# Turning tiles one step ahead, reordering a weight's first sums, and seven block products per expert

## The chip, the cores and the metric

The kernel runs on one core of one Trainium2 chip. The metric is the device time of one launch in microseconds (us). A core has five engines that run side by side, each with its own instruction queue: TensorE (PE) does matrix products and transpositions into PSUM, VectorE (DVE) does elementwise work, ScalarE (ACT) does activations, copies and scalings, GpSimd (POOL) issues the indirect DMAs, and SyncE (SP) issues most of the other DMAs. An engine works through its queue in order; a wait for another engine or a DMA holds everything behind it in that queue.

## What is computed

A state x of 625 tokens by 1024 goes through four layers, each added to x behind a layer norm: a graph layer with eight relations and a gate, a quantized linear layer, a graph convolution, and a mixture of eight experts (top 2) with a shared expert. Cut to what the change touches:

```python
# layer 1: x @ root is the first matrix product of the kernel
out = x @ root + bias
for r in range(8):
    out = out + mean[r] @ weight[r]
...
# layers 2 and 3
acc = x_int8 @ weight_int8.T
h = einsum('nd,od->no', x, W) + b
...
# layer 4
logits = x @ router_w
expert_in = einsum('nec,nh->ech', dispatch, x)
hmid = silu(einsum('ech,ehf->ecf', expert_in, w1) + b1[:, None, :])
expert_out = einsum('ecf,efh->ech', hmid, w2) + b2[:, None, :]
y = einsum('nec,ech->nh', combine, expert_out)
shared = silu(x @ sw1 + sb1) @ sw2 + sb2
out = y + 0.1 * shared
```

An expert has 196 slots, 1024 inputs, 256 hidden values and 1024 outputs; all of this is float32.

## The kernel before

The 625 tokens are five tiles of 125 rows. PE contracts over partitions, so each tile is first turned (`transposed`: eight 128-column blocks in two groups of four; each group goes to a PSUM tile of a ring of two, and ACT copies it to SBUF). Products go to a ring of four PSUM tiles (`mm_tile`), each of which is free again when its reader, on DVE or ACT, is done.

The program is written with a scheduler behind it. It keeps PE's steps in the written order (`issue_after`, `in_steps`), but on the other engines it takes, at each moment of its own planned time, the earliest written instruction that is ready; so a later one can fill a gap. `behind(d, e)` puts d after e on an engine without a wait.

The matrix products of layer 1 use seven block products in place of eight (Winograd's form of Strassen's scheme). A weight is four blocks of 512 by 512, two tiles are a pair, and for a pair `combine_rows` makes the row sums s1, s2, s4 (and puts one difference in place), `combine_weights` makes t1 = b12 - b11, t2 = b22 - t1, t4 = b21 - t2, and `last_weight` puts b22 - b12 in place of b12. The seven products and the sums out of PSUM are in `tile_pair`; the odd fifth tile goes through plain products in `tile_alone`. `posted` lists the DVE operations that must not be overtaken: the weight sums stand behind the last of them. For the root weight, the first one, `combine_rows(0)` stands ahead of `combine_weights` and fills `posted` first. All later units (seven relations, the gate, the last relation) call `combine_weights` and `last_weight` in `unit`. While they run, DVE counts edges and POOL adds the counts to a table in HBM; SP zeroes that table (three transfers of 3 MB at 31.5 us) and loads the weights in a fixed order.

Layers 2 and 3 are steps on PE: `quantized(t)` is the product of layer 2 for tile t with its layer norm on DVE, `columns(t)` turns tile t and multiplies it by W. `neighbours(t)` is the sum over edges with the next norm on DVE, `router(t)` turns tile t and forms its logits. A step that turns a tile and multiplies it at once has PE waiting for the copy on ACT. Then come the slots (which token goes where), the shared expert's output (`shared_out`, five tiles, whose sums go to X and on to `out` through SP), and the experts.

For each expert e: POOL gathers the tokens of its slots (`gather`, two indirect DMAs of 98 rows); PE turns them (`turn`), both halves one after the other; `expert_hidden` is two groups of eight products of 196 columns with an activation on ACT; `expert_out` is 2 by 2 blocks (98 slots by 512 columns) of two accumulated products, one DVE operation each with the gate and the bias that ACT has scaled by the gate (`b2g`), and a store for each 98 slots, an indirect DMA on POOL that adds to `out`. A store waits for those of the previous expert, since it may add to the same rows. Before the change turn(e+1) follows the hidden layer of e and precedes its output. Weights of expert e+3 are loaded when their slot comes free, and `ye`, which the stores read, has two buffers.

Of the kernel before, what the change touches and what calls it, by code (L numbers as in the profile page):

```python
# [8 lines left out]
F32 = mybir.dt.float32  # L9
# [4 lines left out]
AF = mybir.ActivationFunctionType  # L14
# [32 lines left out]
def layers(  # L47
# [383 lines left out]
    def combine_weights(b):  # L431

        t1, t2, t4 = (tp.tile([128, 4, HC], F32, tag=f"t{i}", name=f"t{i}") for i in (1, 2, 4))
        for o, v, w in ((t1, b[0][1], b[0][0]), (t2, b[1][1], t1), (t4, b[1][0], t2)):
            d = nc.vector.tensor_sub(o, v, w)  # L435
            if posted:
                behind(d, posted[-1])
        return t1, t2, t4
# [54 lines left out]
    def last_weight(b):  # L493

        nc.vector.tensor_sub(b[0][1], b[1][1], b[0][1])
# [31 lines left out]
    combine_rows(0)  # L527
    root_t = combine_weights(root_w)
# [432 lines left out]

    def columns(t):
        transposed(xT, t * P, th[t], P)
        for h in range(2):
            hs = slice(h * HC, (h + 1) * HC)
            ps = mm_tile()
            for k in range(KD):
                last = nc.tensor.matmul(  # L968
                    ps[:P, :],
                    xT[:, k, t * P : (t + 1) * P],  # L970
                    gcn_w[h][k // 4][:, k % 4, :],
                    start=(k == 0),
                    stop=(k == KD - 1),
                )
            z = work.tile([P, HC], F32, tag="z", name="z")
            nc.vector.tensor_add(z, ps[:P, :], gcn_b_row[:, hs])
            nc.scalar.mul(parts[t][0][:, hs], z, dis[:, t : t + 1])
            if not exact:
                hi, lo = (v[:, hs] for v in parts[t])
                nc.vector.scalar_tensor_tensor(  # L980
                    lo, z, dis[:, t : t + 1], hi.bitcast(F32), op0=ALU.mult, op1=ALU.subtract
                )
        return last

    for step, t in ((quantized, 0), (quantized, 1), (quantized, 2), (columns, 0), (quantized, 3),
                    (columns, 1), (quantized, 4), (columns, 2), (columns, 3), (columns, 4)):
# [74 lines left out]
    def router(t):  # L1061
        transposed(xT, t * P, th[t], P)
# [37 lines left out]
    def in_steps(steps):  # L1100
        nonlocal pe_last
        for step, arg in steps:
# [5 lines left out]
            (neighbours, 0), (neighbours, 1), (neighbours, 2), (router, 0), (neighbours, 3),  # L1108
            (router, 1), (neighbours, 4), (router, 2), (shared_hidden, (0, 0, 3 * P)),
            (router, 3), (router, 4), (logits, None), (shared_hidden, (1, 0, 3 * P)),  # L1110
# [124 lines left out]
    done, base = sent, []  # L1235

    def shared_out(t):
        for h in range(2):
            hs = slice(h * HC, (h + 1) * HC)
            ps = mm_tile()  # L1240
            for f in range(2):
# [9 lines left out]
            nc.vector.scalar_tensor_tensor(  # L1251
                X[t][:, hs], z, 0.1, X[t][:, hs], op0=ALU.mult, op1=ALU.add
# [11 lines left out]
    in_steps([(shared_out, t) for t in range(NT)])  # L1264
# [36 lines left out]
    def turn(e):  # L1301
        for j in range(2):
            last = transposed(tiles["xeT"][e % 2], j * CP, rows_of_slots(e, j), CP)
        return last

    def expert_hidden(e):
        for f in range(2):
            ps = mm_tile()
            for k in range(KD):
                last = nc.tensor.matmul(  # L1310
                    ps[:, :CAP],
                    weights[e][0][:, k, f * 128 : (f + 1) * 128],
                    tiles["xeT"][e % 2][:, k, :],
                    start=(k == 0),
                    stop=(k == KD - 1),
                )
            nc.scalar.activation(
                tiles["he"][e % 2][:, f, :], ps[:, :CAP], AF.Silu, bias=b1_sb[:, e, f : f + 1]
            )
        return last  # L1320

    sent = base

    def expert_out(e):
        nonlocal sent
# [3 lines left out]
        for j in range(2):  # L1329
# [3 lines left out]
            for h in range(2):  # L1333
# [13 lines left out]
                in_halves = e == NE - 1 and j == 1  # L1347
                if h == 0 and not in_halves:
                    continue

                if in_halves:
                    to, v, rows = out.rearrange("n (h c) -> (n h) c", h=2), ye[:, j, hs], 2 * N
                    at = bass.IndirectOffsetOnAxis(ap=half_i[:, h : h + 1], axis=0)
                else:
                    to, v, rows, at = out, ye[:, j, :], N, rows_at(j, e, token_i)
                d = nc.gpsimd.indirect_dma_start(  # L1356
                    out=to,
                    out_offset=at,
                    in_=v,
                    in_offset=None,  # L1360
                    bounds_check=rows - 1,
                    oob_is_err=False,
                    compute_op=ALU.add,
                )
                for o in sent:
                    tc.declare_no_dep(d.ins, o.ins, reason="a token has one slot of an expert")
                after(d, earlier)
                sent.append(d)
        return last

    gather(0)
    for e in range(4):
        load_weights(e)
        load_bias(e)
    gather(1)
    in_steps(((turn, 0),))
    for e in range(NE):
# [5 lines left out]
        in_steps(((expert_hidden, e),))  # L1383
        if e + 2 < NE:
            gather(e + 2)
        in_steps((*(((turn, e + 1),) if e + 1 < NE else ()), (expert_out, e)))
# [58 lines left out]
```

## Time and profile before

| | us |
|---|---|
| median of three runs (1214.35 to 1215.61) | 1215.44 |
| the profiled execution | 1218.88 |
| its span on the core | 1217.1 |

| stage (us from the span's start) | what runs |
|---|---|
| 0 to 84 | tile norms and the root weight |
| 84 to 641 | eight relations and the gate |
| 641 to 835 | sums over edges |
| 835 to 1010 | gate, layers 2 and 3 |
| 1010 to 1068 | sums over edges, router |
| 1068 to 1094 | slots, shared expert's output |
| 1094 to 1217 | eight experts |

How to read the profile: a line in order of time has its start, its duration, the engine, the line of the kernel, the operation, what it writes and reads by name, the shapes and a count of merged instructions; in brackets stands the idle time before it and what ended it. A product in float32 appears as two records. PEld is the loading of PE's stationary operand. A line of waits has the total, the number and the longest. A line of a stretch has its length, the busy time and count of PE, PEld, DVE, ACT and POOL, the clock that TensorE was granted (1.00 is full speed), and the DMA's busy share and GB/s.

### The profile page before, as it was taken

What the parts mean: (1) busy time and instruction counts of PE and PEld (TensorE: products, weight loads), DVE (VectorE), ACT (ScalarE), POOL (GpSimd) and SP (SyncE); (2) the same over time, 40 slices, a digit from 0 to 9 for tenths busy, and PEclk for the clock granted to TensorE, in tenths of its full rate; (3) what the DMA queues carried; (4) which work ended last, traced back from release to release, by engine and by line L of the source; (5) the groups of instructions that cost most, each with busy time, mean ns of one, the idle gap of its engine ahead of it and who ended that gap; (6) DMA issues with size and microseconds to landing.
All of it is one profiled execution on the core that took longest, in us unless ns stands there. A gap on an engine that the chain in (4) does not pass through costs nothing.

```text
span 1217.1 us, 10940 instructions
## 1 busy us (share of the span) xinstructions
PE 1183.8 (97%) x3770; PEld 647.6 (53%) x3770; DVE 836.4 (69%) x1292; ACT 172.8 (14%) x308; POOL 485.5 (40%) x224
## 2 busy tenths in 40 slices
PE   6899999999999999999999999999999999999996
PEld 3344444444444444444447888786445447756663
DVE  5789797888897979793427888874998516451111
ACT  2000000000000000000013122213321111213331
POOL 1003888888787889888700000002420000013322
PEclk9999999999999999999999999999999999989998
DMA  8986737373646364636347779804540006269962
GB/s 274 268 232 153 204 60 202 65 196 74 183 85 174 88 178 92 155 70 149 50 106 197 172 192 257 218 1 115 147 142 17 18 26 212 82 213 267 284 156 43
DMA packets 156009, 177.05 MB, mean 145 GB/s; under 512 B 78831, under 2 KB 95590, under 8 KB 155946
## 3 DMA queue, kind: packets, MB, share of 16 engines
q1 hardware_dynamic: 66082, 132.03, 37.5%
q0 software_dynamic: 72864, 12.01, 10.3%
q10 hardware_dynamic: 17000, 32.24, 8.5%
q8 instruction: 32, 0.52, 0.2%
q14 instruction: 31, 0.25, 0.1%
HBM read 131.66 MB, written 45.50 MB: 146 GB/s over the span
## 4 chain that ended last, share of the span: by engine, by line
PE 92%; DMA 2%; ACT 2%; DVE 1%; issue 1%; POOL 1%; POOLq 0%; ACTq 0%; DVEq 0%
PE mm L442 51%; PE mm L684 15%; PE mm L968 6%; PE mm L812 6%; PE mm L1337 3%; PE mm L1310 2%; PE mm L996 2%; PE mm L1242 2%; PE mm L945 1%; PE mm L1079 1%; PE tr L186 1%; DMA out_dram<-aT,token_i 1%; ACT xT L189 1%; PE lgT L1066 1%; POOL out_dram L1356 1%
## 5 line engine op out<-in xcount | busy, mean ns | idle before, releaser
L400 POOL DMA_INDIRECT table<-hits,idx x165 | 409.6, 2483 | 195.7 <-DMA table<-zero 103.4
L442 PE MATMUL mm<-w,xT 128*125 128x512 f32 x800 | 351.1, 593 | 0.0
L376 DVE SCALAR_TENSOR_TENSOR junk<-kr,key,wm 125x1375 f32<-125x1375 f32 x165 | 271.5, 1646 | 1.1
L442 PEld LDWEIGHTS mm<-w,xT 128*125 128x125 f32 x800 | 150.3, 188 | 192.4 <-issue 190.0
L684 PE MATMUL mm<-hi,b 125*125 125x512 f32 x400 | 157.8, 394 | 0.0
L442 PE MATMUL mm<-t,btot 128*125 128x512 f32 x320 | 145.6, 598 | 4.5 <-DVE t L435 4.5
L684 PE MATMUL mm<-y,b 125*125 125x512 f32 x350 | 138.7, 396 | 0.0
L442 PEld LDWEIGHTS mm<-t,btot 128*125 128x125 f32 x320 | 60.6, 189 | 83.2 <-issue 77.7
L1294 POOL DMA_INDIRECT th<-tokens,token_i x16 | 16.2, 1010 | 208.7 <-DMA w<-in_L_ffn_w_dram 171.2
L1018 POOL IOTA io<- 125x40 f32 x1 | 0.2, 198 | 225.2 <-ACT th L794 225.2
L745 DVE SCALAR_TENSOR_TENSOR X<-mm,rc,X 125x512 f32<-125x512 f32 x80 | 60.0, 751 | 38.7 <-PE mm L684 37.9
L684 PEld LDWEIGHTS mm<-hi,b 125*125 125x125 f32 x400 | 74.2, 186 | 18.4 <-issue 0.2
L684 PEld LDWEIGHTS mm<-y,b 125*125 125x125 f32 x350 | 64.9, 185 | 15.8
L442 PE MATMUL mm<-w,btot 128*125 128x512 f32 x160 | 71.9, 592 | 0.0
L442 PE MATMUL mm<-t,xT 128*125 128x512 f32 x160 | 71.9, 592 | 0.0
L968 PE MATMUL mm<-w,xT 128*125 128x512 f32 x160 | 70.0, 595 | 1.4 <-ACT xT L189 1.4
L812 PE MATMUL mm<-w,xT 128*125 128x512 f32 x160 | 69.1, 592 | 0.0
L560 ACT CAST hi<-y 125x512 fp32r<-125x512 f32 x80 | 44.1, 617 | 159.8 <-PE mm L684 113.3
L1337 PE MATMUL mm<-w,th 128*98 128x512 f32 x128 | 56.3, 592 | 0.0
L461 ACT COPY y<-mm 125x512 f32<-125x512 f32 x18 | 10.6, 586 | 299.9 <-PE mm L442 292.1
L435 DVE TENSOR_TENSOR t<-w,t 128x2048 f32<-128x2048 f32 x20 | 45.8, 2290 | 6.9 <-DMA w<-in_L_gnn_weight_dram 6.5
L442 PEld LDWEIGHTS mm<-t,xT 128*125 128x125 f32 x160 | 29.9, 188 | 38.2 <-issue 37.7
(207 smaller groups left out, 1197.0 us busy)
## 6 DMA issues: line engine op xcount, KB each, us to landing
w<-in_L_gnn_weight_dram SPq DMA_DIRECT2D x32, 1024.0 KB
w<-in_L_ffn_w_dram SPq DMA_DIRECT2D x16, 1024.0 KB
yd<-y ACTq DMA_DIRECT2D x70, 224.0 KB
y<-yd SPq DMA_DIRECT2D x70, 224.0 KB
table<-zero SPq DMA_DIRECT2D x4, 3054.0 KB
b<-table SPq DMA_DIRECT2D x8, 1367.2 KB
kr<-key_rows ACTq DMA_DIRECT2D x15, 601.6 KB
w<-in_L_gnn_w_gate_dram SPq DMA_DIRECT2D x8, 1024.0 KB
```

The lines of the kernel that those rows point to most:

```text
L376: d = nc.vector.scalar_tensor_tensor(junk, kr, key[:, c : c + 1], wm[:, (EG - 1 - j) * P : (2 * EG - 1 - j) * P], op0=ALU.is_equal, op1=AL ...
L400: d = nc.gpsimd.indirect_dma_start(out=table, out_offset=bass.IndirectOffsetOnAxis(ap=idx[:, c : c + 1], axis=0), in_=hits[:, c : c + 1], ...
L435: d = nc.vector.tensor_sub(o, v, w)
L442: last = nc.tensor.matmul(ps[:P, :], lhs[:, k], rhs[:, k], start=(start and k == 0), stop=(stop and k == 3))
L560: upper.append(nc.scalar.copy(hi, y))
L684: last = nc.tensor.matmul(ps[:P, :], counted[r][:, k, t * P : (t + 1) * P], part, start=(k == ks[0] and part is parts[r, h, k][0]), stop=( ...
L745: nc.vector.scalar_tensor_tensor(X[at][:, hs], v[:P, :], rc[:, r, at : at + 1], X[at][:, hs], op0=ALU.mult, op1=ALU.add,)
L812: last = nc.tensor.matmul(ps[:P, :], xT[:, 4 * i + k, t * P : (t + 1) * P], gate_w[h][i][:, k, :], start=(i == 0 and k == 0), stop=(i == 1 ...
L968: last = nc.tensor.matmul(ps[:P, :], xT[:, k, t * P : (t + 1) * P], gcn_w[h][k // 4][:, k % 4, :], start=(k == 0), stop=(k == KD - 1),)
L996: last = nc.tensor.matmul(ps[:P, :], aT[:, k, t * P : (t + 1) * P], part[:, h * HC : (h + 1) * HC], start=(k == 0 and part is parts[k][0]) ...
L1242: last = nc.tensor.matmul(ps[:P, :], hT[:, f, t * P : (t + 1) * P], sw2_w[:, f, hs], start=(f == 0), stop=(f == 1),)
L1337: last = nc.tensor.matmul(ps[:CP, :], he[:, f, j * CP : (j + 1) * CP], weights[e][1][:, f, hs], start=(f == 0), stop=(f == 1),)
```

## The change

At the root weight, t1 and t2 are written ahead of the row sums of the first pair, so that they stand behind nothing posted; t4 and the last weight sum stay behind the row sums. In every unit, the last weight sum is now also written behind the last posted operation.

In layers 3 and 4, turning a tile becomes a step of its own, and is written one step ahead of the product that reads it, except for the first. Tiles 2 and 3 of the router are turned one after the other.

Expert 0's gather is written ahead of the shared output, and its two turns among the tiles of that output. Each later expert's turn is split: one half behind each half of the hidden layer before it.

The output of experts 0 to 6 uses seven block products: four blocks of the hidden values (two halves of the slots by two halves of the 256) and four of w2 (two halves of 256 by two of 1024). The weight sums (`expert_sums`) are made once an expert is done for the next, behind the last DVE operation of the shared output, in two sets of buffers in xT, which is free by then. ACT copies the first product out of PSUM, DVE makes three sums, and each of the four output blocks takes two DVE operations (`gated`), one of which reads PSUM. Both scaled biases are made first. The second half of the slots is stored first. Expert 7 keeps the old form, its second half stored in two parts as before.

```diff
-    def combine_weights(b):
+    def combine_weights(b, beside=None):
         t1, t2, t4 = (tp.tile([128, 4, HC], F32, tag=f"t{i}", name=f"t{i}") for i in (1, 2, 4))
         for o, v, w in ((t1, b[0][1], b[0][0]), (t2, b[1][1], t1), (t4, b[1][0], t2)):
+            if o is t4 and beside is not None:
+                combine_rows(beside)
             d = nc.vector.tensor_sub(o, v, w)
...
-        nc.vector.tensor_sub(b[0][1], b[1][1], b[0][1])
+        behind(nc.vector.tensor_sub(b[0][1], b[1][1], b[0][1]), posted[-1])
...
-    combine_rows(0)
-    root_t = combine_weights(root_w)
+    root_t = combine_weights(root_w, 0)
     last_weight(root_w)
...
+    def turned(t):
+        return transposed(xT, t * P, th[t], P)
+
     def columns(t):
-        transposed(xT, t * P, th[t], P)
...
-    for step, t in ((quantized, 0), (quantized, 1), (quantized, 2), (columns, 0), (quantized, 3),
-                    (columns, 1), (quantized, 4), (columns, 2), (columns, 3), (columns, 4)):
+    for step, t in ((quantized, 0), (quantized, 1), (quantized, 2), (turned, 0), (columns, 0),
+                    (turned, 1), (quantized, 3), (columns, 1), (turned, 2), (quantized, 4),
+                    (turned, 3), (columns, 2), (turned, 4), (columns, 3), (columns, 4)):
...
     def router(t):
-        transposed(xT, t * P, th[t], P)
...
-            (neighbours, 0), (neighbours, 1), (neighbours, 2), (router, 0), (neighbours, 3),
-            (router, 1), (neighbours, 4), (router, 2), (shared_hidden, (0, 0, 3 * P)),
-            (router, 3), (router, 4), (logits, None), (shared_hidden, (1, 0, 3 * P)),
+            (neighbours, 0), (neighbours, 1), (neighbours, 2), (turned, 0), (neighbours, 3),
+            (router, 0), (turned, 1), (neighbours, 4), (router, 1), (turned, 2), (turned, 3),
+            (router, 2), (shared_hidden, (0, 0, 3 * P)), (turned, 4), (router, 3), (router, 4),
+            (logits, None), (shared_hidden, (1, 0, 3 * P)),
...
-    in_steps([(shared_out, t) for t in range(NT)])
...
-    def turn(e):
+    def turn(ej):
+        e, j = ej
+        return transposed(tiles["xeT"][e % 2], j * CP, rows_of_slots(e, j), CP)
+
+    def expert_hidden(ef):
+        e, f = ef
...
+    def expert_sums(e):
+        w = weights[e][1]
+        b11, b12, b21, b22 = (w[:, i, h * HC : (h + 1) * HC] for i in range(2) for h in range(2))
+        t1, t2, t4 = (in_xT((3 * (e % 2) + i) * HC, HC) for i in range(3))
+        for o, v, x in ((t1, b12, b11), (t2, b22, t1), (t4, b21, t2), (b12, b22, b12)):
+            d = nc.vector.tensor_sub(o, v, x)
+            behind(d, written[-1])
+        return t1, t2, t4
...
+    def expert_out_in_seven(e):
+        nonlocal sent
+        ye, he = (tiles[v][e % 2] for v in ("ye", "he"))
+        b2_row, w = tiles["b2"][e], weights[e][1]
+        t1, t2, t4 = expert_t[e]
+        earlier, sent = sent, []
+        a11, a21, a12, a22 = (he[:, f, j * CP : (j + 1) * CP] for f in range(2) for j in range(2))
+        s1, s2, s3, s4 = (in_xT(6 * HC + (4 * (e % 2) + i) * CP, CP) for i in range(4))
+        nc.vector.tensor_add(s1, a21, a22)
+        nc.vector.tensor_sub(s2, s1, a11)
+        nc.vector.tensor_sub(s3, a11, a21)
+        nc.vector.tensor_sub(s4, a12, s2)
+        p1, u2 = (in_xT(6 * HC + 8 * CP + i * HC, HC)[:CP, :] for i in range(2))
+        u3 = work.tile([P, HC], F32, tag="z", name="z")[:CP, :]
+        b2g = []
         for j in range(2):
+            gate_of = slots[:, j, e, 2:3]
+            b2g.append(work.tile([P, D], F32, tag="xn", name="xn")[:CP, :])
+            nc.scalar.mul(b2g[j], b2_row, gate_of)
...
+        def gated(j, h, u, ps):
...
+            nc.vector.scalar_tensor_tensor(o, u, gate_of, b2g[j][:, hs], op0=ALU.mult, op1=ALU.add)
+            nc.vector.scalar_tensor_tensor(o, ps, gate_of, o, op0=ALU.mult, op1=ALU.add)
+
+        b = [w[:, i, h * HC : (h + 1) * HC] for i in range(2) for h in range(2)]
+        nc.scalar.copy(p1, product(a11, b[0]))
+        gated(0, 0, p1, product(a12, b[2]))
+        nc.vector.tensor_add(u2, product(s2, t2), p1)
+        nc.vector.tensor_add(u3, product(s3, b[1]), u2)
+        ps = product(s1, t1)
+        nc.vector.tensor_add(u2, ps, u2)
+        gated(1, 1, u3, ps)
+        gated(1, 0, u3, product(a22, t4))
+        store(e, out, rows_at(1, e, token_i), ye[:, 1, :], N, earlier)
+        gated(0, 1, u2, product(s4, b[3]))
+        store(e, out, rows_at(0, e, token_i), ye[:, 0, :], N, earlier)
+        return last
...
     gather(0)
+    in_steps(
+        (*((shared_out, t) for t in range(3)), (turn, (0, 0)), (shared_out, 3), (turn, (0, 1)), (shared_out, 4))
+    )
...
-    in_steps(((turn, 0),))
+    expert_t = {0: expert_sums(0)}
     for e in range(NE):
...
-        in_steps(((expert_hidden, e),))
+        for f in range(2):
+            in_steps(((expert_hidden, (e, f)),))
+            if e + 1 < NE:
+                in_steps(((turn, (e + 1, f)),))
         if e + 2 < NE:
             gather(e + 2)
-        in_steps((*(((turn, e + 1),) if e + 1 < NE else ()), (expert_out, e)))
+        in_steps(((expert_out if e == NE - 1 else expert_out_in_seven, e),))
+        if e + 1 < NE - 1:
+            expert_t[e + 1] = expert_sums(e + 1)
```

`store` is the indirect DMA of the old `expert_out`, put in a function of its own, and `product` a single 128-deep matmul into a new PSUM tile.

More of the change, by code (lines that the diff above doesn't have):

```diff
@@ L1234, in layers @@
     b2_first = [work.tile([P, D], F32, tag="gx", name="gx") for _ in range(2)]
-    done, base = sent, []
+    done, base, written = sent, [], []
     def shared_out(t):
@@ L1250, in shared_out @@
             nc.vector.tensor_add(z, ps[:P, :], sb2_row[:, hs])
-            nc.vector.scalar_tensor_tensor(
-                X[t][:, hs], z, 0.1, X[t][:, hs], op0=ALU.mult, op1=ALU.add
+            written.append(
+                nc.vector.scalar_tensor_tensor(
+                    X[t][:, hs], z, 0.1, X[t][:, hs], op0=ALU.mult, op1=ALU.add
+                )
             )
@@ L1299, in rows_of_slots @@
         return th[2 * (e % 2) + j][:CP, :]
-    def turn(e):
[L1302 to L1318, printed above, removed]
-            )
+    def turn(ej):
+        e, j = ej
+        return transposed(tiles["xeT"][e % 2], j * CP, rows_of_slots(e, j), CP)
@@ L1320, in expert_hidden @@
+    def expert_hidden(ef):
+        e, f = ef
+        ps = mm_tile()
+        for k in range(KD):
+            last = nc.tensor.matmul(
+                ps[:, :CAP],
+                weights[e][0][:, k, f * 128 : (f + 1) * 128],
+                tiles["xeT"][e % 2][:, k, :],
+                start=(k == 0),
+                stop=(k == KD - 1),
+            )
+        nc.scalar.activation(
+            tiles["he"][e % 2][:, f, :], ps[:, :CAP], AF.Silu, bias=b1_sb[:, e, f : f + 1]
+        )
         return last
@@ L1322, in layers, with in_xT @@
     sent = base
+    free_xT = xT.rearrange("p k n -> p (k n)")
+    def in_xT(c, n):
+        return free_xT[:, c : c + n]
+    def expert_sums(e):
[6 more added lines that the diff above has]
+        return t1, t2, t4
@@ new lines, in store, with product @@
+    def store(e, to, at, v, rows, earlier):
+        d = nc.gpsimd.indirect_dma_start(
+            out=to,
+            out_offset=at,
+            in_=v,
+            in_offset=None,
+            bounds_check=rows - 1,
+            oob_is_err=False,
+            compute_op=ALU.add,
+        )
+        for o in sent:
+            tc.declare_no_dep(d.ins, o.ins, reason="a token has one slot of an expert")
+        after(d, earlier)
+        sent.append(d)
+    def expert_out_in_seven(e):
[13 more added lines that the diff above has]
+        b2g = []
+        for j in range(2):
+            gate_of = slots[:, j, e, 2:3]
+            b2g.append(work.tile([P, D], F32, tag="xn", name="xn")[:CP, :])
+            nc.scalar.mul(b2g[j], b2_row, gate_of)
+        last = None
+        def product(lhs, rhs):
+            nonlocal last
+            ps = mm_tile()
+            last = nc.tensor.matmul(ps[:CP, :], lhs, rhs, start=True, stop=True)
+            return ps[:CP, :]
+        def gated(j, h, u, ps):
+            gate_of = slots[:, j, e, 2:3]
+            hs = slice(h * HC, (h + 1) * HC)
+            o = ye[:, j, hs]
+            nc.vector.scalar_tensor_tensor(o, u, gate_of, b2g[j][:, hs], op0=ALU.mult, op1=ALU.add)
[13 more added lines that the diff above has]
+        return last
@@ L1346, in expert_out @@
                 )
-                in_halves = e == NE - 1 and j == 1
+                in_halves = j == 1
                 if h == 0 and not in_halves:
@@ L1351, in expert_out @@
                 if in_halves:
-                    to, v, rows = out.rearrange("n (h c) -> (n h) c", h=2), ye[:, j, hs], 2 * N
                     at = bass.IndirectOffsetOnAxis(ap=half_i[:, h : h + 1], axis=0)
+                    store(e, out.rearrange("n (h c) -> (n h) c", h=2), at, ye[:, j, hs], 2 * N, earlier)
                 else:
[L1355 to L1368, printed above, removed]
+                    store(e, out, rows_at(j, e, token_i), ye[:, j, :], N, earlier)
         return last
     gather(0)
+    in_steps(
+        (*((shared_out, t) for t in range(3)), (turn, (0, 0)), (shared_out, 3), (turn, (0, 1)), (shared_out, 4))
+    )
     for e in range(4):
```

## The prediction

> **What bounds the kernel now.** I read the page's busy table and chain of waits first, then the waits of PE, then the order of time in the places that the diff touches.
>
> ```profile
> PE 1183.8 (97%) x3770; PEld 647.6 (53%) x3770; DVE 836.4 (69%) x1292; ACT 172.8 (14%) x308; POOL 485.5 (40%) x224
> ...
> PE 92%; DMA 2%; ACT 2%; DVE 1%; issue 1%; POOL 1%; POOLq 0%; ACTq 0%; DVEq 0%
> ...
> PE mm L442 <- DVE t L435: 4.5, 1, 4.5
> PE tr L186 <- ACT flat L189: 2.0, 8, 0.3
> ...
> PE mm L968 <- ACT xT L189: 1.4, 5, 0.4
> PE lgT L1066 <- ACT xT L189: 1.2, 5, 0.2
> ```
>
> PE is the bound, and the edits can only win what PE does too much or waits for: one long wait at the root weight, and a short wait at each transposition whose copy PE needs at once. In order of time, the root:
>
> ```profile
> 31.50 2.29 DVE L435 TENSOR_TENSOR t<-w 128x2048 f32<-128x2048 f32 x1
> ...
> 33.83 2.29 DVE L435 TENSOR_TENSOR t<-w,t 128x2048 f32<-128x2048 f32 x1
> ...
> 36.17 5.40 PE L442 MATMUL mm<-t,btot 128*125 128x512 f32 x8 [4.49 <-DVE t L435]
> ...
> 30.00:40.00 10.00, 5.51 (x9) 2.00 (x8) 10.00 (x8) 0.59 (x1) 0.00 (x0) 0.83 1.04 283
> ```
>
> The second line's result releases the third. The last line is a stretch of ten us: its last figure but two is the granted clock, 0.83 where its neighbours have 1.00. The eight matmuls after the wait took 5.24 us from 36.17 to 41.41, elsewhere 3.43 (a row of 3.60 less its tail). So this wait costs 4.49 us and 1.81 us of slow clock. One expert of the last stage:
>
> ```profile
> 1142.94 0.94 PE L186 MATMUL tr<-ident,th 98*128 98x98 f32 x8 [0.24 <-ACT flat L189]
> ...
> 1143.72 7.03 PE L1337 MATMUL mm<-w,th 128*98 128x512 f32 x16
> ...
> 1149.53 1.55 POOL L1356 DMA_INDIRECT out_dram<-btot,token_i  x1 [4.23 <-DMA out_dram<-aT,token_i]
> ...
> 1150.59 5.50 PE L1310 MATMUL mm<-flat,w 128*128 128x196 f32 x32
> ...
> 1150.79 0.75 DVE L1344 SCALAR_TENSOR_TENSOR btot<-mm,slots,xn 98x512 f32<-98x512 f32 x1 [0.91 <-PE mm L1337]
> ```
>
> Such a period is 14.06 us (L1337 starts at 1129.66, 1143.72, 1157.79), all PE: 16 records of L1337 at 0.43, 32 of L1310, 16 of transposition, and one wait in the middle of the transpositions. DVE has only four operations of 0.75 there. The first store waits for the landing of the previous expert's.
>
> **Root weight.** t1 and t2 now stand before the row sums and behind nothing posted. t1 needs the third block of the root weight, t2 the fourth. Estimate of their landing: DMA moves 129, 337, 298, 400, 318, 276 GB/s in the first six stretches of 4 us, and the blocks end at 4.4 and 5.95 MB of the queue's order, so at about 15.5 and 20 us. DVE is idle from 15.8 to 20.56 (waits 4.76 for the key transposition) and from 26.2 to 29.0 (2.82 for a copy): each holds one subtraction of 2.29. Queued behind a t1 that waits are the key copy and tile 1's normalization, which ended at 24.4; PE needs it at 26.8, so 2.4 us are free. The row sums then run at 29.01, the first two are done at 30.5, and PE asks for its second product at 31.7. t4 and the last subtraction follow, done at about 36.3; the product that needs the latter starts at 38.6, t4 is needed later. Gain 6.3 if both fit; bounds: 0 if the order stays, and 1.9 less than the full gain if both land in tile 1's normalization. I take 6.3, since both gaps lie under other waits. After it, PE has no idle time until 640, so the gain must survive what comes late next: unit 0's weights. Three of them queue behind the zeroing of the table, whose 9.2 MB are through at about 69 (at 265 GB/s from 31.5), so land at about 73 to 79, and PE would ask at 78.0, 81.5, 84.9. The fourth is loaded when PE frees its slot, so moves along. At 613.6 the counts are loaded when POOL is done, at 628 the DMA is idle, and PE would want them at 634. The same order on all later units ("last subtraction behind the last posted") costs nothing: its own PE reader comes after that posted add anyway.
>
> **Transpositions ahead.** Columns: waits of 0.42, 0.30, 0.24, 0.24, 0.24 before L968. The first stays (turned directly ahead); the others get a step in between: gain 1.0. Their inputs are early enough: tile 4 is normalized at 970.4, its turn comes at about 979. Router: five waits of 0.24 go, but tiles 2 and 3 are now turned back to back, through two PSUM tiles: the third group waits for a copy (0.58 after 0.2), about 0.4. Gain 0.8. In both, ACT gets the same copies, in another order. Shared output: the gather of expert 0 now precedes it, at the same 1073.2, since POOL waits for the slots; landings of 6.4 and 7.1 put it at 1081.6, and the turn is asked for at about 1084.5. The waits of 0.24 and 0.19 and their issue go: gain 0.5. The later tiles' stores to out on SP move back by 0.8, and the bias loads behind them, which are needed 20 us later.
>
> **Seven products.** Per expert PE loses one product, two records at 0.43: 0.86. Turning expert e+1 is split around the second half of the hidden layer, so the wait between its two halves goes: 0.24 by PE's rows, 0.43 by the weight loads' (0.81 from 1141.70, next 1142.94); I take 0.35. Together 1.2, seven times: 8.5 (bounds 7.7 and 9.0). That makes the period about 12.8.
>
> The cover: DVE's new work. Per expert, with durations of rows: four sums of 128x98 at 0.24 (a 125x40 operation's spacing), eight gate operations at 0.75 (L1344; SBUF alone 0.69, L1251), three sums out of PSUM at 0.69 (L480), four weight sums of 128x512 at 0.69 (L1250): 1.0 + 6.0 + 2.1 + 2.8 = 11.8 against 12.8. It fits, with 1 us. Walked from the end of the hidden layer (0): ACT has the activation at 0.6; s1, s2 at 0.75 to 1.25; product 3, their reader, starts at 2.5. Product 1 ends at 1.7, its ACT copy at 2.5, the first gate pair at 4.1; product 6 wants that PSUM tile (one of four) at 5.1. The sum that frees product 3's tile ends at 4.7, wanted at 5.9; the next at 5.4, wanted at 6.8. No PE wait, with 1 us of slack each. The two bias products on ACT (1.15 each) now both precede that copy; they can run when their two tiles come free, 2.6 us before 0 and earlier. If they stood behind the activation, the copy would end at 4.6 and product 6 wait 1.1.
>
> **Stores.** The stores of an expert come at 9.0 and 10.9 after 0, 1.85 apart, where they were 2.4 to 2.8 apart. A pair waits for the landing of the pair before: 1.85 + 10.7 (landings 9.6 to 11.3 while weights are loaded) + 0.9 from landing to issue = 13.4 > 12.8, so they fall behind by some 0.6 per expert while the DMA is full (share 0.95 to 1.08 from 1100 to 1164). PE feels it only when a store is more than 6.5 us late (ye has two buffers). The gathers, in the same POOL queue, wait for a turn that ends ahead of the stores, and land 10 us before they are read. With landings of 6.3 at the end the stores catch up; still the last pair but one is issued until T-1.3 (T, end of the last hidden layer), lands at T+5.0, and the last expert's first store goes at T+5.9 where it went at T+4.7 (1202.80 less 1198.12). Loss 1.2, bounds 0 and 4; I take 1.5 for longer issue (below).
>
> **Sum.** 6.3 + 1.0 + 0.8 + 0.5 + 8.5 - 1.5 = 15.6 us. The profiled execution's 1218.88 (span 1217.1) becomes 1203.3; the median of the three runs is 3.4 below it, so **1199.8 us**.
>
> **A rule against the change.** Beside DVE operations with two SBUF inputs (L376, 1.64 us) POOL's issues L400 take 2.5 to 4.03 us, and 1.98 where DVE is idle; L376 itself keeps to 1.635 to 1.703. So I lengthen stores, by some 0.3 in the sum, and DVE not at all. The Trainium skill, SBUF — State Buffer, section "SBUF: two separate sides", says more: GpSimd and a DVE operation with two SBUF inputs lock a shared port pair against each other for a whole instruction. By that, DVE would be held too, and the sum would be rival D.
>
> **Rivals.**
> A, the forecast.
> E, the stores become a bound: with 0.6 more per issue, the pair's cycle is 14.6; 1.8 late per expert over five is 9, of which 6.5 is free; 2.6 come back in each of the last two, and the end is 3.5 later than in A: 1203.3. For it: the store already waits 4.23 for a landing. Against: issues of 1.52 to 1.56 throughout.
> F, the order of DVE at the root leaves the wait: 1206.1. For it: DVE's order comes from the scheduler, which fills gaps by its own clock. Against: nothing holds t1 back any more.
> C, the expert stage keeps its period (1 us of slack on DVE eaten by the order on ACT or DVE, so that PE waits for PSUM): the 8.5 go, 1208.3. C and F together: 1214.6.
> D, the other side: in the expert stage DVE is held through POOL's two stores (1.54) and two gathers (1.0) of each expert: 11.8 + 5.1 = 16.9 per expert, 2.8 above the old period, seven times 19.9: 1215.4 - 8.6 + 1.5 + 19.9 = 1228. It decides from a DVE load of 15.1. For it: twelve of the nineteen new operations read SBUF twice, where the old four read PSUM. Against: L376's durations. This is the rule of the Trainium skill, SBUF — State Buffer, that is named above.
> That xT's parts, reused for sums, are ordered as one whole: L426 writes btot at 58.07 while PE reads its other part (56.85 to 60.45), so I give it nothing.
>
> **Chances.** A 0.53, E 0.10, F 0.07, C 0.14, C with F 0.05, D 0.11. Faster (by over 0.2%, 2.4 us, about what three runs spread over 1.3 us can tell): A, E, F, C, 0.84; within: 0.05; slower: D, 0.11. A's own range is 1195.5 to 1203.5, from its bounds (root 4.4 to 6.3, experts 7.7 to 9.0, waits up to 1 more, end 0 to 4). From 1195 to 1209 it holds A, E, F and C.
>
> **What would show it.** L442 after the root's first product: no wait on t, eight records in 3.6, clock 1.0 at 30 to 40. L968 and L1066: waits on xT's copies gone but for the first and one between tiles 2 and 3. In the expert stage 14 records of products, hidden layers 12.8 apart, DVE busy some 11 of them; PE waiting on DVE or ACT there speaks for C; DVE operations longer beside POOL's for D; the last pair of stores later against the last hidden layer for the end. Wrong altogether if hidden layers stay 14 us apart, or if PE waits for unit 0's weights at 78.

## The result

| | median of the runs, us | ratio to the kernel before, 95% interval |
|---|---|---|
| before (4 runs, 1214.35 to 1215.61) | 1215.43 | |
| after (4 runs, 1202.12 to 1205.65) | 1203.62 | 0.9903 [0.989, 0.9916] |
| after, measured again beside three of the experiments (4 runs, 1198.09 to 1200.23) | 1199.01 | 0.9861 [0.9842, 0.988] |

The change makes the kernel faster, by 11.8 us in the first measurement. 1199.8 was forecast: 3.8 less than the first median, 0.8 more than the second. The first median lies 0.1 above the range that the prediction gives its own forecast, and almost on the number of rival E (1203.3). The first profile of the changed kernel (an execution of 1204.37, span 1202.6) shows what was forecast in most places and one large loss. Its busy table (busy us, share, instructions) and the first lines of PE's waits (total, times, longest):

```profile
PE 1171.7 (97%) x3756; PEld 642.6 (53%) x3756; DVE 890.9 (74%) x1397; ACT 175.3 (15%) x315; POOL 489.1 (41%) x224
```

```profile
PE tr L186 <- DVE X L171: 9.3, 1, 9.3
PE mm L444 <- DMA w<-in_L_gnn_weight_dram: 2.4, 1, 2.4
PE tr L893 <- ACT aT L896: 1.4, 3, 0.6
PE mm L1387 <- DVE aT L1396: 1.0, 1, 1.0
```

The waits on t and on most of the copies are gone. Two have come: one for a weight of unit 0, one for a gate operation of an expert. (The chain of waits of this profile breaks off after its last two pieces, so it isn't read here.) The root and unit 0 in order of time, and three stretches (the last figure but two is the granted clock):

```profile
16.92 2.29 DVE L437 TENSOR_TENSOR t<-w 128x2048 f32<-128x2048 f32 x1 [0.72 <-DMA w<-in_L_gnn_root_dram]
24.86 2.28 DVE L437 TENSOR_TENSOR t<-w,t 128x2048 f32<-128x2048 f32 x1
31.96 3.60 PE L444 MATMUL mm<-t,btot 128*125 128x512 f32 x8
80.89 19.10 PE L444 MATMUL mm<-w,xT 128*125 128x512 f32 x40 [2.41 <-DMA w<-in_L_gnn_weight_dram]
```

```profile
30.00:40.00 10.00, 10.00 (x24) 4.33 (x24) 9.96 (x15) 0.58 (x1) 0.00 (x0) 1.00 1.03 283
80.00:84.00 4.00, 3.11 (x5) 1.48 (x6) 0.65 (x3) 0.00 (x0) 0.00 (x0) 0.72 1.01 318
84.00:88.00 4.00, 4.00 (x9) 1.65 (x8) 1.71 (x1) 0.00 (x0) 0.00 (x0) 0.86 1.10 383
```

t1 stands in DVE's first gap; t2 runs just ahead of the second and moves the next tile's statistics into it. The second product starts at once, eight records take 3.60, and the clock is full from 30 to 40. Then PE reaches unit 0 at 78, its weight isn't there, and the clock falls: 0.28 x 4 + 0.14 x 4 = 1.7 us more. One expert period in order of time:

```profile
1136.18 2.83 PE L1315 MATMUL mm<-flat,w 128*128 128x196 f32 x16
1146.73 0.75 DVE L1395 SCALAR_TENSOR_TENSOR aT<-xT,slots,xn 98x512 f32<-98x512 f32 x1 [3.00 <-DMA out_dram<-aT,token_i]
1147.52 1.55 POOL L1348 DMA_INDIRECT out_dram<-btot,token_i  x1 [9.03 <-DVE aT L1395]
1148.39 1.10 PE L1387 MATMUL mm<-xT,th 128*98 128x512 f32 x2 [1.04 <-DVE aT L1396]
1149.37 0.99 POOL L1300 DMA_INDIRECT th<-tokens,token_i  x1 [0.30 <-issue]
1150.18 2.83 PE L1315 MATMUL mm<-flat,w 128*128 128x196 f32 x16
1150.66 1.54 POOL L1348 DMA_INDIRECT out_dram<-btot,token_i  x1 [0.30 <-DVE xT L1342]
```

Hidden layers start 12.72 us apart, but for this one period of 14.00: DVE may not write ye before an older store has landed, PE waits for DVE. Between the two stores of an expert POOL now issues a gather.

Where the time went, stage by stage, as differences of starts in the profile of before (span 1217.1) and in the two profiles of after (spans 1202.6 and 1196.4), us gained:

| stage | forecast | first profile | second |
|---|---|---|---|
| 0 to the sums over edges (before 640.12) | 6.3 | 1.66 | 5.18 |
| from there to layer 2's products (before 918.62) | 0 | 1.37 | 1.37 |
| columns and router, to the slots (before 1067.93) | 1.8 | 3.37 | 3.37 |
| slots, shared output, to the first hidden layer (before 1094.18) | 0.5 | 2.50 | 4.20 |
| experts, to the last one's output (before 1198.12) | 8.5 | 8.24 | 8.80 |
| end | -1.5 | -2.64 | -2.22 |
| sum | 15.6 | 14.50 | 20.70 |

Not all of it is the change. The profiled execution of before was 3.4 us above its median, and two of its stretches ran at a low clock: 0.72 and 0.85 at 912 to 920 (0.28 x 4 + 0.15 x 4 = 1.7 us), and 0.85, 0.50, 0.80 at 1068 to 1080 (3.4 us). By its row the first of these cost 1.37: root_alone, at full clock there, takes the same 277.15 as both profiles of after, where before takes 278.50. That leaves 15.9 of the 20.70 (less 1.37 and 3.4), with the weight of unit 0 in time.

### The profile page after: what moved, and what is told of

It is laid out like the page before. It is cut to its first block, busy times and chain, and to the rows that moved or that the text cites. A ratio compares the mean times of both kernels' runs of the same rounds, so it can differ in the third digit from the quotient of the medians.

```text
span 1202.6 us, 11037 instructions
## 1 busy us (share of the span) xinstructions
PE 1171.7 (97%) x3756; PEld 642.6 (53%) x3756; DVE 890.9 (74%) x1397; ACT 175.3 (15%) x315; POOL 489.1 (41%) x224
## 5 line engine op out<-in xcount | busy, mean ns | idle before, releaser
L444 PEld LDWEIGHTS mm<-w,btot 128*125 128x125 f32 x160 | 30.0, 188 | 38.2 <-issue 38.2
```

Of the source, the lines that this page charges most:

```text
L444: last = nc.tensor.matmul(ps[:P, :], lhs[:, k], rhs[:, k], start=(start and k == 0), stop=(stop and k == 3))
```

## The experiments

In all of them what is not named is unchanged. Medians stand beside 1215.34, 1215.43 and 1215.12 of the kernel before in the three groups (chips 11, 11 and 3).

**The changed kernel again** (after_again).

> The changed kernel once more, beside the three variants of it, on their chip: 1203.6 us (ratio to the kernel before 0.990). In its profile unit 0's first product waits some 2.4 us for its weight at 78 to 81, and one expert's products wait some 1.3 us for a DVE operation that itself waits for a store's landing. If that second wait were a chance of the one execution, it would be absent here.

1199.01 us, ratio 0.9861 [0.9842, 0.988]. Here the weight is in time: PE goes on at 79.14 without a wait, at full clock. The expert's wait is there again, 0.5 us, in a period of 13.46: it is no chance.

**The third zeroing transfer behind the weights** (zero_later).

```diff
-        for c in (0, 12, 24):
+        for c in (0, 12):
             clear_table(c)
...
         if r == 0 and not exact:
+            clear_table(24)
             clear_table(36)
```

> The changed kernel with the third zeroing transfer issued behind unit 0's four weights in place of ahead of them. Theory: the zeroing alone makes the weights late, so with 6.1 MB ahead of them in place of 9.2 MB they land by about 65 and PE's wait of 2.4 us at 78 goes, and with it the slow clock behind it (0.72 and 0.86 in two stretches of 4 us, together 1.7 us): 4.1 us faster than the changed kernel, 1199.5, with the clock at 1.00 from 80 to 88. Rival 1: the weights wait for their buffers and not for the zeroing, so that the wait and the time stay, 1203.6. Rival 2: the third transfer now holds up the first additions on POOL (103 us) and the counts come late at 634, so that the 4.1 us are lost again there.

1198.55 us, 0.9864 [0.9843, 0.9885], with one of six runs at 1204.70: as after_again, which had no wait to lose, so the time tells nothing. (The chip does not decide that: root_alone and dve_loaded, below, ran later on the same one and had the wait.) Two stretches, zero_later and then after_again (the last two figures are the DMA's share and GB/s):

```profile
64.00:72.00 8.00, 8.00 (x20) 3.50 (x19) 5.25 (x8) 0.00 (x0) 0.00 (x0) 1.00 0.54 199
72.00:80.00 8.00, 8.00 (x20) 3.57 (x19) 6.71 (x9) 0.00 (x0) 0.00 (x0) 1.00 0.19 75
```

```profile
64.00:72.00 8.00, 8.00 (x20) 3.54 (x19) 5.01 (x8) 0.00 (x0) 0.00 (x0) 1.00 1.05 212
72.00:80.00 8.00, 8.00 (x21) 3.41 (x20) 6.95 (x9) 0.00 (x0) 0.00 (x0) 1.00 0.99 344
```

With one transfer fewer the DMA is nearly idle ahead of 79; with three it is full up to the moment PE asks.

**The root's order alone** (root_alone): the kernel before, with t1 and t2 ahead of the row sums and the last weight sum behind the last posted operation.

```diff
-    combine_rows(0)
-    root_t = combine_weights(root_w)
+    root_t = combine_weights(root_w, 0)
```

> The kernel before with the new order at the root weight alone. Theory: the wait of 4.5 us and the slow clock behind it (1.8 us) go, and all of it lasts if unit 0's first weight lands before PE asks for it at 78 to 79, as in the second profile of the changed kernel: 6.3 us faster than before, 1209.0. If that weight comes as late as in the first profile (asked at 78.0, first product at 80.9, clock 0.72 and 0.86), 4.1 us are given back: 1213.2. Rival: the order of DVE alone gains nothing, 1215.3.

1215.97 us, 0.9996 [0.9984, 1.0008]: nothing is gained. Unit 0 in before, and here:

```profile
84.32 17.33 PE L442 MATMUL mm<-w,xT 128*125 128x512 f32 x40
```

```profile
84.27 19.15 PE L444 MATMUL mm<-w,xT 128*125 128x512 f32 x40 [6.24 <-DMA w<-in_L_gnn_weight_dram]
```

The 4.49 us come back as 6.24, and the 40 products take 19.15 in place of 17.33 by the slow clock.

**The root's order with the third transfer moved** (root_zero_later): both diffs above on the kernel before.

> The kernel before with the new order at the root weight, which alone gained nothing, and the third zeroing transfer behind unit 0's weights. Theory: the weights then land before 76 where PE asks at some 78, so the whole of the root's gain lasts: 6.1 to 6.3 us, 1209.2. Rival: something behind the root (a later unit, the counts at 634) takes the gain whatever the weights do: 1215.4.

1208.73 us, 0.9949 [0.9935, 0.9962]: 6.4 gained. Unit 0 (the view ends at 90, so it counts 27 of the 40):

```profile
78.57 11.75 PE L444 MATMUL mm<-w,xT 128*125 128x512 f32 x27
```

The two kernels differ in the place of one DMA (and ran on two chips, each beside its own kernel before). So it is the zeroing, and not a wait for the weights' buffers, that made them late.

**All zeroing ahead of the weights** (zero_all_first).

```diff
-        for c in (0, 12, 24):
+        for c in (0, 12, 24, 36):
...
-        if r == 0 and not exact:
-            clear_table(36)
```

> The changed kernel with all four zeroing transfers ahead of unit 0's weights, where three were. Theory: these weights land when the zeroing is through; 3.05 MB more at some 265 GB/s are 11.5 us, so that the first lands at about 90 where PE asks at 79: a wait of some 11 us and 1.7 us of slow clock behind it, 12 to 13 us slower than the changed kernel, 1211 to 1212. With one transfer fewer ahead of them they landed before 76. Rival: the weights wait for their buffers, the number of transfers ahead of them does nothing: 1199.

1220.64 us, 1.0038 [1.0024, 1.0052]: 21.6 more than after_again, where 12 to 13 were expected. Its profile is that of its slowest run, 1226.20.

```profile
98.73 19.59 PE L444 MATMUL mm<-w,xT 128*125 128x512 f32 x40 [19.83 <-DMA w<-in_L_gnn_weight_dram]
```

The direction is the theory's; the size is not, since the DMA was slower as well. Summed over seven stretches of 8 us from 24 to 80, it moved 14.6 MB in after_again, 14.2 in the first profile of after, 13.4 in root_alone and 13.4 here, at a share of 1.0 from 32 on in all of them. 1.2 MB at 250 GB/s are 5 us: as much as the first products at 79.1, 80.9 and 84.3 are apart. A nearer measure than after_again is dve_loaded (below), which has three transfers and ran in the same group: zero_all_first takes 12.6 more than it, though dve_loaded carries added DVE work.

**Turning ahead alone** (turns_alone): the kernel before, with `turned` as a step of its own in the two lists of layers 3 and 4, as in the change.

```diff
     def columns(t):
-        transposed(xT, t * P, th[t], P)
...
     def router(t):
-        transposed(xT, t * P, th[t], P)
```

> The kernel before with the transpositions of layers 3 and 4 (columns and router) one step ahead, and nothing else. The prediction has 1.0 and 0.8 us for these, from the waits that the rows of PE name: 1213.5. The two profiles of the whole change had 2.1 and 1.3 there: 1211.9. If the larger figures are real, the distance from the start of a tile's transposition to the start of its first product must be 0.9 where a step stands between and some 1.3 where none does, so that more goes than the named wait of 0.24. If they come from a clock that happened to be lower in the one profile, the smaller figures hold.

1212.71 us, 0.9981 [0.997, 0.9992]: 2.7 less than before, between the two expectations; the stage decides. Between layer 2's products and the slots (919.07 to 1065.01) it takes 145.94, as in both profiles of after, against 149.31: 3.37. A tile of the columns in before, and in turns_alone:

```profile
980.09 1.02 PE L186 MATMUL tr<-ident,th 125*128 125x125 f32 x8
981.35 14.00 PE L968 MATMUL mm<-w,xT 128*125 128x512 f32 x32 [0.24 <-ACT xT L189]
```

```profile
980.33 1.02 PE L186 MATMUL tr<-ident,th 125*128 125x125 f32 x8
981.19 19.05 PE L970 MATMUL mm<-w,xT 128*125 128x512 f32 x44
```

From the start of the turn to the first product it is 1.26 with a wait and 0.86 without: the row names 0.24 of the 0.40. The 32 products after a wait take 14.00 in place of 13.90, so a tile loses 0.50.

**The old output for all experts** (products_plain).

```diff
-        in_steps(((expert_out if e == NE - 1 else expert_out_in_seven, e),))
-        if e + 1 < NE - 1:
-            expert_t[e + 1] = expert_sums(e + 1)
+        in_steps(((expert_out, e),))
...
-                in_halves = j == 1
+                in_halves = e == NE - 1 and j == 1
```

> The changed kernel with the old form of the output (eight block products, no sums) for all eight experts; the transpositions stay split and ahead. Theory: a product is worth its two records, so hidden layers start 12.72 + 0.86 = 13.58 us apart, which costs 6.0 us over seven experts; in return the end goes back to some 19.0 us behind the last output's first product (2.6 less) and expert 4's wait of 1.3 us is gone: 6.0 - 2.6 - 1.3 = 2.1 us slower than the changed kernel, 1205.7. Rival: the seven products are the whole of the expert stage's gain, the split transpositions are worth nothing: period 14.06, 5.5 us slower than the changed kernel, 1209. Other rival: the stores were no burden, the end stays where it is with the changed kernel: 1208.3.

1201.28 us, 0.9883 [0.9864, 0.9902]: 2.3 more than after_again. Hidden layers are 13.58 us apart (1107.46, 1121.05, 1134.63), the experts take 100.43 where after_again took 95.14, and the end 18.88 (1199.6 less 1180.72) where it took 21.2. So a product is worth 0.86, the split turn 14.06 - 13.58 = 0.48 per expert; and of the 6.0 us that seven products save, 2.3 are paid back at the end and 0.7 in one expert's wait.

**Gathers behind both stores** (gathers_behind).

```diff
-            nc.gpsimd.indirect_dma_start(
+            d = nc.gpsimd.indirect_dma_start(
                 out=rows_of_slots(e, j), out_offset=None, in_=tokens, in_offset=rows_at(j, e, token_i)
             )
+            if e - 4 in stored:
+                behind(d, stored[e - 4])
...
+        stored[e] = sent[-1]
```

> The changed kernel with the gathers of expert e+4 held behind both stores of expert e, where one of them stood between the stores. Theory: the second store then goes 1.3 us earlier, a pair's cycle falls from 15.5 to some 14.2 us, still above the period of 12.72, but the delay that adds up by expert 2 falls under what ye's two buffers allow, so expert 4's wait of 1.3 us goes; the end keeps its place against the last hidden layer. 1.3 us faster than the changed kernel, 1202.3. Rival: the store waits for a DMA that is full, an earlier issue lands no earlier, the cycle stays at 15.5 and the wait stays: 1203.6.

1198.12 us, 0.9867 [0.9843, 0.9891]; the profiled execution is as long as after_again's (spans 1196.5 and 1196.4). The stores keep up now (first stores at 1096.0, 1109.6, 1122.3, 1136.0) and no longer hold DVE. But:

```profile
1131.77 0.69 DVE L1346 TENSOR_TENSOR xT<-w 128x512 f32<-128x512 f32 x1 [1.74 <-DMA w<-in_L_ffn_w_dram]
1132.38 0.68 DVE L1408 TENSOR_TENSOR xT<-mm,xT 98x512 f32<-98x512 f32 x1
1135.10 2.94 PE L1319 MATMUL mm<-flat,w 128*128 128x196 f32 x16 [0.28 <-DVE btot L1400]
```

A weight sum of the next expert stands in DVE's queue ahead of the sum that frees a PSUM tile, and waits for its weight. The period is 13.45. One wait has taken the place of another.

**More work on DVE** (dve_loaded): t1, t2 and t4 of experts 0 to 6 are made twice.

```diff
-        for o, v, x in ((t1, b12, b11), (t2, b22, t1), (t4, b21, t2), (b12, b22, b12)):
+        for o, v, x in (
+            (t1, b12, b11), (t2, b22, t1), (t4, b21, t2),
+            (t1, b12, b11), (t2, b22, t1), (t4, b21, t2), (b12, b22, b12),
+        ):
```

> The changed kernel in which three of the four weight sums of experts 0 to 6 are made twice, with the same result: three more DVE operations of 128x512 per expert. The prediction adds up durations, 11.8 us of DVE work per expert in a period of 12.8; by that, 2.1 more are 13.9, DVE becomes the bound and the period rises by 1.1: 6 to 7 us slower, 1205.5. By the rows of the changed kernel such operations start 0.60 apart where they last 0.69, and DVE is idle for 2.0 of 12.72 us: 1.8 more just fit, and the time rises by 1 us at most, 1199 to 1200.

1208.03 us (5 runs from 1204.60 to 1212.39), 0.9935 [0.9912, 0.9959]. The time is not DVE's: in its profile unit 0's weight was 4.18 us late, with slow clock behind it. The stage is clean: from the first hidden layer to the last output 96.68 (1088.68 to 1185.36) against 95.14. Of the 1.5 us, one wait has all:

```profile
1127.64 0.69 DVE L1345 TENSOR_TENSOR xT<-w 128x512 f32<-128x512 f32 x1 [1.96 <-DMA w<-in_L_ffn_w_dram]
1128.25 0.68 DVE L1405 TENSOR_TENSOR z<-mm,xT 98x512 f32<-98x512 f32 x1
1128.99 2.94 PE L1315 MATMUL mm<-flat,w 128*128 128x196 f32 x16 [1.77 <-DVE z L1405]
```

The other periods are 12.7 to 12.8: 1.8 us more of DVE work per expert fit. (zero_all_first, without the added work, takes 97.07 in this stage, by waits for a weight and for the landing of a store.)

**Weight sums held, and all of this together** (held): zero_later and gathers_behind, and

```diff
-            behind(d, written[-1])
+            behind(d, held_by.get(e - 1, written[-1]))
...
-        gated(1, 0, u3, product(a22, t4))
+        held_by[e] = gated(1, 0, u3, product(a22, t4))
```

> The changed kernel with the third zeroing transfer behind unit 0's weights, the gathers behind both stores, and the weight sums of an expert held, on DVE, behind the gate operations of the expert before (they stood ahead of them in two runs and waited there for a weight, 1.7 and 2.0 us, with sums behind them that PE needed). Theory: no wait at unit 0, hidden layers 12.72 us apart throughout, 94.4 us from the first to the last output (95.1 to 95.7 in the changed kernel): 1197.5 where the clock is full, and a few runs up to 5 us above where it is not. Rival: with the stores earlier, weights land later and the wait stays some 0.7 us in another place: 1198.1.

1201.52 us (1198.13 to 1202.81), 0.9873 [0.9857, 0.989]. Unit 0 and the experts are as expected (PE goes on at 77.75 without a wait, all periods are 12.72, and it is 94.41 from the first hidden layer to the last output), the time isn't:

```profile
636.29 0.47 PE L686 MATMUL mm<-lo,b 125*125 125x512 f32 x1 [2.18 <-DMA b<-table]
```

POOL ended its additions to the table at 624.7, where it ended at 608.6 to 613.6 in after and after_again, and PE, earlier now, waited for the counts, with 1.7 us of slow clock behind it (0.64 and 0.93 from 636 to 644). That is the loss that the second rival of zero_later named; why it comes here and not in zero_later stays open (last section).

**One tile of the shared output between the slots' products** (held_split): held, with

```diff
-    in_steps(((fill_slots, 0), (fill_slots, 1)))
+    in_steps(((fill_slots, 0), (shared_out, 0), (fill_slots, 1)))
...
-        (*((shared_out, t) for t in range(3)), (turn, (0, 0)), (shared_out, 3), (turn, (0, 1)), (shared_out, 4))
+        (*((shared_out, t) for t in (1, 2)), (turn, (0, 0)), (shared_out, 3), (turn, (0, 1)), (shared_out, 4))
```

> The kernel of the run beside it (held), with one tile of the shared output between the two halves of the products that find the tokens of the slots. These 40 products of 24 columns run for 3.6 us in one piece; in the profiles of some runs the granted clock then falls to 0.50 to 0.60 for a few us. Theory: two pieces of 1.8 us do not bring it down: no clock under 1.00 between 1050 and 1085 in the profile, and the runs some 5 us above the others (a quarter so far) are gone or rarer; the median falls by 0 to 1 us. Rival: those runs have another cause, and their share stays.

1199.43 us (1198.29 to 1200.81), 0.9864 [0.9849, 0.9879]. It has the wait for the counts too (2.0 us). The stretch behind the slots' products in the profiles of before, held and held_split:

```profile
1072.00:1076.00 4.00, 4.00 (x6) 1.63 (x6) 1.30 (x8) 1.15 (x1) 2.21 (x3) 0.50 1.01 376
```

```profile
1064.00:1068.00 4.00, 4.00 (x9) 1.95 (x9) 1.23 (x8) 1.15 (x1) 2.03 (x2) 0.60 1.05 393
```

```profile
1064.00:1068.00 4.00, 4.00 (x27) 2.77 (x26) 2.54 (x5) 0.24 (x1) 2.11 (x2) 1.00 1.04 387
```

In two pieces there is no fall. after_again's profile has none with one piece either, so that alone proves little. But held and held_split can be compared closely: the last section counts the clock's steps, and the products begin 0.24 us behind the start of a step in held and 0.07 us behind one in held_split. There the split is what differs. It is one pair of profiles.

**The old output for expert 6 too** (held_split_plain6): held_split, with the old form for experts 6 and 7.

```diff
-        in_steps(((expert_out if e == NE - 1 else expert_out_in_seven, e),))
+        in_steps(((expert_out if e >= NE - 2 else expert_out_in_seven, e),))
...
-        if e + 1 < NE - 1:
+        if e + 1 < NE - 2:
...
-                in_halves = j == 1
+                in_halves = e == NE - 1 and j == 1
```

> The same (held, split), with the old form of the output for expert 6 as well as for expert 7. Theory: its two stores go some 3 us earlier against its products, so the last expert's do not wait for their landing: the end takes 18.9 us from the last output's first product in place of 21.0, against one product more, 0.86: 1.2 us faster than the run beside it (held_split), 1196.3. Rival: the end is set by the last expert's own stores, and the product is lost: 0.9 slower.

1196.85 us (1195.47 to 1198.13), 0.9847 [0.9833, 0.9861], the fastest kernel here: its interval lies below the first one of the change, and overlaps the second. The 2.6 us to held_split are mostly the wait for the counts, which this profile doesn't have. Of its own the edit has little: the end is 21.0 (1195.1 less 1174.09) against 22.0, and the product costs 0.86, so 0.2 in place of 1.2. The last stores on POOL:

```profile
1171.75 1.52 POOL L1355 DMA_INDIRECT out_dram<-aT,token_i  x1 [6.46 <-DMA out_dram<-btot,token_i]
1173.58 1.52 POOL L1355 DMA_INDIRECT out_dram<-aT,token_i  x1 [0.30 <-issue]
1180.98 1.52 POOL L1355 DMA_INDIRECT out_dram<-btot,token_i  x1 [5.88 <-DVE btot L1440]
```

Expert 6's output is ready earlier, but its first store still waits for expert 5's landing: it goes 2.3 us ahead of the last expert's first product (1174.09), where it went 2.1 ahead in held_split (1174.90, 1176.96). The chain of all the stores, not the form of one expert's output, sets the end.

## Why the forecast held, and where it didn't

**Root, 6.3.** What it says of DVE and PE was right: both subtractions ahead of the row sums, no wait, full clock, so rival F was not seen. (The second profile's 5.18 is less since PE's first products began 1.3 us later than in before, 29.35 to 28.09.) The step that failed is "Three of them queue behind the zeroing of the table, whose 9.2 MB are through at about 69 (at 265 GB/s from 31.5), so land at about 73 to 79, and PE would ask at 78.0". In the six profiles with three transfers ahead of it and PE that early, it was there when PE asked, at 79.1 to 79.5, in three, and PE went on at 80.9, 83.0 and 84.3 in the others; with two transfers it was there in all five, for PE asking as early as 77.75. The prediction had named a wait for unit 0's weights at 78 as a sign of being "Wrong altogether"; in the first profile that sign came. The rate was taken as one number, and it varies from execution to execution; the estimate's late end lay 1 us beyond the need, and was not priced. In before, this lateness was covered by the very wait that the change removes: PE asked at 84.32. root_alone (nothing gained) and root_zero_later (6.4) show it. In the first profile it cost 2.41 + 1.7 of the 6.3.

**Columns and router, 1.8.** Right mechanism, too small: 3.37, by turns_alone. The working took the waits that the rows name; a wait costs from start to start, 0.50 per tile in the columns. The single wait foreseen between tiles 2 and 3 is there (0.24 at 1035.22).

**Shared output, 0.5.** With the slow clock left out it is 0.8: 22.05 in after_again against 22.87 in root_zero_later, which has the old order and full clock there.

**Experts, 8.5.** 8.24 and 8.80. The period came out at 12.72 (12.8). The product is worth 0.86 as said, the split turn 0.48 where 0.35 was taken; one expert's wait takes 1.28 or 0.74 of it. The walk through the PSUM tiles and ACT's order was right: rival C, the unchanged period, was not seen, nor C with F.

**DVE's cover.** "11.8 against 12.8. It fits, with 1 us" was too strict: consecutive DVE operations of 0.69 start 0.60 apart, DVE is idle for 2.0 us of a period, and dve_loaded put 1.8 more there.

**Stores, and rival E.** The delay of a store over ye's two buffers, with PE waiting, is E's mechanism in the place that it named, but smaller: one wait, since stores catch up once no weights are loaded. The pair's cycle was 15.5 where the forecast had 13.4 and E 14.6, because a gather (0.98 and 0.30) went between the two stores; that the gathers "wait for a turn that ends ahead of the stores" did not keep them from there. The end lost 2.2 to 2.6 where 1.5 was taken (bounds 0 and 4).

**Rival D, the lock.** Not seen on DVE's side. In after's expert stage operations with two SBUF inputs (L1395, L1342) last 0.74 to 0.75 and 0.68 to 0.69 beside POOL's stores as elsewhere; POOL's store is lengthened, 1.52 to 2.39 (3.84 once in held_split). By the Trainium skill, SBUF — State Buffer, section "SBUF: two separate sides", whichever starts first holds the port pair and the other is blocked; these rows show only POOL blocked.

**The sum.** Four errors of size have different signs: root -1.1 and -4.6 in the two profiles (-6.3 in root_alone), columns and router +1.6, shared output and experts up to +0.6, end -0.7 to -1.1. The gains of 11.8 and 16.3 lie on both sides of the 15.6 forecast, and which one came hung on one weight's landing. That the time came within 4 us rests on this too, which is luck, not on every term being right. Nor does 1203.62 beside E's 1203.3 speak for E: most of the 6.2 us between the two profiles of after, 2.41 + 1.7 at unit 0 and 1.7 of slow clock behind the slots' products, is not E's. The upper end of A's range does not follow from its own bounds: these, added up (root 4.4, experts 7.7, end 4), reach 1205.0 and not 1203.5.

## What to carry to other kernels

A wait that an edit removes was also time that let a transfer land: before pricing the gain, find the next thing that arrives late, and give its arrival the spread of the DMA's rate, not its mean. Price a PE wait from start to start against the same steps without it, not by the wait's own row. When a queue holds work for a later stage, ask what stands behind an operation whose input may be late, and put it behind what the present stage needs.

## What the runs showed that was not expected

PE can be busy and still lose its clock. The 40 products of 24 columns that find the slots' tokens run without a gap for 3.4 to 3.9 us where they stand in one piece. In five of these twelve profiles (before, after, held, dve_loaded, zero_all_first) the granted clock then fell to half, for 3.41 us in three and 6.83 in two (1.7 and 3.4 us lost); in the other seven it stayed at 1.00. What tells them apart is when the products begin. In the record of the clock, in all 14 profiles, once the clock is full each change comes a whole number of steps of 3.41 us behind the one before, so the steps can be counted on to these products. In the five, one step held 2.88 to 3.23 us of the products, and the fall came at its end; in the seven, no step held more than 2.50. The Trainium skill, TensorE: Matmul & The Clock Gate, section "Part 1: The HAM clock gate (the "warmup" mystery)", tells of a free-running window of about 3.4 us of PE activity that sets the clock to half or full. The twelve profiles agree with that; that so thin a product counts as idle is what they suggest, and no run here changes its width. A wait of 2.41 us already cost 1.7 us of clock behind it, and one of 2.0 in held_split did too, less than the idle window of that page.

The rate of a full DMA varied between executions of the same transfers: from 32 to 72 at a share of 1.0 it moved 206 to 294 GB/s in one, 199 to 291 in another. In all it moved 10.2, 10.7 and 10.9 MB (five stretches of 8 us) in the three profiles whose weight was in time (after_again, gathers_behind, products_plain), and 9.7 to 10.0 in the three where it was late. Why is open. So is why POOL's additions ended 11 us later in held and held_split than in the three other kernels with the third transfer moved: by 200 us POOL had made 26 in these two, 29 in the three, 28 to 32 in before and in both profiles of after, and the distance stayed.
